# Table entries traced behind the first half of the scores, and the last tile but one taken down before the last goes up

## The chip, the cores and the metric

The kernel runs as one program on one core of one Trainium2 chip. The metric is the device time of one execution in microseconds (us); for a kernel it is given as the median of its runs. Before the change the median of three runs is 1698.82 us (1694.02 to 1705.58). The execution that was profiled is a run of its own: it took 1695.92 us, of which the span from the first to the last instruction is 1694.1 us.

## The reference, cut to what matters

One layer of a hybrid model in float32, on x of shape (2, 2048, 256):

```python
x = x + mamba(layernorm(x))        # state-space mixer; not touched by the change
x = x + ffn(layernorm(x))          # 8 experts, each token goes to 2 of them
x = x + attention(layernorm(x))    # 16 heads of 64
x = x + ffn(layernorm(x))          # the same experts again

def attention(x, w_qkv, w_out, ln_w, ln_b):   # cut
    x_in = layer_norm(x, ln_w, ln_b)
    q, k, v = split(x_in @ w_qkv.T)
    attn = softmax(einsum('ibnd,jbnd->ijbn', q, k) / sqrt(256), axis=1)
    return x + einsum('ijbn,jbnd->ibnd', attn, v) @ w_out.T

def ffn(x, Wr, br, Wl1, bl1, Wl2, bl2):       # cut
    s = x @ Wr.T + br                          # router: best 2 of 8, weights from a softmax
    a, b = split(x @ Wl1[e] + bl1[e])          # for each chosen expert e
    y = (silu(a) * b) @ Wl2[e] + bl2[e]        # summed with the two weights
```

Attention runs over the first axis of x, which has length 2: every token attends to itself and to the token at the same place in the other sequence. A softmax over two values is a sigmoid of their difference, and that is how the kernel computes it.

## The kernel before, in words

**Stages.** In order of time: the mixer with the routing and the first tiles of the first expert layer (to about 741 us), the remaining tiles of the first expert layer (tiles named `_f`, to about 897 us), attention together with the routing and the first tiles of the second expert layer (tiles named `_g` and, for the early ones, `_ge`; to about 1408 us), and the remaining tiles of the second expert layer (to the end at 1694.1 us).

**Experts.** The class `Experts` serves both expert layers: `ffn` for the first, whose results are added into `resid`, and `last` for the second, whose results are added into the output. For each group of 512 tokens, `prepare` takes the layer norm, writes the tokens (`acc`, L316) and their normalized rows (`xnd`, L318) to memory through the SP queue, and works out which expert slots each token gets. `enter` then writes one table row of three numbers for each token and slot by indirect DMAs on POOL: 16 "free" blocks once (L420, the first time only), and 8 blocks for each group (L433), each block being 128 rows. Each entry may not be issued before the last POOL instruction named by `pool(...)` (`tc.issue_after(on_pool[0])`), and the entries of L433 wait for all 16 free ones. When some groups are in, `plan_early` decides on VectorE (DVE) which expert tiles are already full, and `early` may run those before all groups are in. A tile is 256 tokens of one expert; a half tile is 128.

**One expert tile.** `fetch` has SP load the table rows (L656) and the expert's weights and biases (L668 to L674), and POOL gathers the tokens (L683). `turn` transposes the tokens on TensorE (PE; L709) and copies them on ScalarE (ACT; L713). `up` runs four parts (`up_part`: matmuls at L722, a silu on ACT at L730, a product on DVE at L731 into `gT`). `down` multiplies `gT` with the second weight (L754), takes bias and gate into `y` (ACT L766, DVE L767) and adds the two halves of `y` to memory by indirect DMAs on POOL (L778); between the two halves a gather of a later tile or a small memset (L777) is issued. `by` (L766) has one buffer, the banks of `down` (tag C) are two.

**The late tiles** are run by `run`. In its loop tile i goes up, tile i+1 is turned, and tile i-1 is taken down. At its end, with n the number of tiles, the last tile goes up in four parts and the last but one is taken down between part 1 and part 2 (`between`), then the last is taken down. In the second expert layer the last but one is a full tile, in the first it is a half tile.

**Attention** works on four steps s of 512 tokens in each of the two sequences. For each s: `front` (layer norms and transposes), `scores` (eight pieces of query and key products, L1337, with DVE products and sums at L1356 and L1357), `weights` (sigmoid, transposition `ppt` at L1372, a store of the probabilities to memory at L1377 and eight loads `o<-prob` of 512 KB each, which spread them over the partitions, L1383), `mix` (value products `pvd`, L1411, each multiplied on DVE with `o`, L1419) and `outward` (output products `pao`, L1431, added to x on DVE, L1439). The first half of `scores(s+1)` stands between `weights(s)` and `mix(s)`, the second half behind `outward(s)`.

**What sets the order.** The side work (`front`, `prepared`, `entered`) are generators in a list, `aside.waiting`; the main loop takes a few steps of the first one in the list at fixed places (`aside.step`). A generator that has to wait spins there: `front(s+2)` yields without work until `mix(s)` has been traced, and while it does, nothing behind it in the list moves. What is written this way is the order in which the program is traced. In attention only the SP queue keeps that order; on PE, DVE, ACT and POOL a planner lists the instructions ahead of time: of those that are ready by its own estimates, the one traced first goes first. In `run`, POOL, ACT and DVE keep the written order too, and only PE is listed by the planner.

For each s the list gets, behind what it still holds, the generator `entered()`, which writes the table entries of all groups that are routed by the time it is reached, and plans early tiles behind the fourth and the sixth group. Groups are numbered 1 to 8, two for each s.

Of the kernel before, what the change touches and what calls it, by code (L numbers as in the profile page):

```python
# [46 lines left out]
def kernel(  # L47
# [35 lines left out]
    def bank(tag, name):  # L83
        return ps.tile([P, 512], F32, tag=tag, name=name)
# [140 lines left out]
    aside = Aside()  # L225
# [54 lines left out]
    class Experts:  # L280
# [451 lines left out]
                t["gT"][:, i, :n], p[:, n : 2 * n], t["b1"][:, NHT + i : NHT + i + 1], sa[:, :n], ALU.add, ALU.mult  # L732
            )

        def up(self, i, between=None):
            t = self.ts[i]
            nm = t["nm"]
            pool = fe if i % 2 else self.f2
            t["gT"] = pool.tile([P, NHT, TT], F32, tag="gT", name=f"gT_{nm}", bufs=1)
            for j in range(NHT):  # L740
                self.up_part(t, j, "AB"[j % 2])
                if between is not None and j == 1:
                    between()

        def down(self, i, tag, then):
            t = self.ts.pop(i)
# [67 lines left out]
        def run(self):  # L814
            ahead = 3
            first = next(i for i, t in enumerate(self.seq) if not t[4])
            n = len(self.seq)
            with (
                tc.tile_pool(name=f"f2{self.name}", bufs=2) as self.f2,
                tc.manual_schedule(  # L820
                    engines={mybir.EngineType.Pool, mybir.EngineType.Activation, mybir.EngineType.DVE}
                ),
            ):
                self.fetch(first + ahead + 1, first + ahead)
                self.turn(first)
                assert self.seq[-1][1] == 2
                for i in range(first, n - 1):
                    self.fetch(i + ahead + 2, i + ahead + 1, gather=False)
                    if i == first + 6:
                        with tc.manual_schedule(engines={mybir.EngineType.PE}):  # L830
                            beyond = nc.values_load(self.beyond[0:1, 0:1], min_val=0, max_val=NHF - NIN)
                            self.up(i)
                    else:
                        self.up(i)
                    self.turn(i + 1)
                    if i > first:
                        self.down(i - 1, "C", i + ahead)
                    else:
                        for h in range(2):
                            self.gather(i + ahead, h)  # L840
                    if i == first + 2:
                        yield
                self.up(n - 1, lambda: self.down(n - 2, "C", None))
                self.down(n - 1, "C", None)
                with tc.If(beyond > 0):
                    for tile in self.more:
                        i = len(self.seq)
                        self.seq.append(tile)
                        self.fetch(i + 1, i + 1)
                        self.turn(i)  # L850
                        self.up(i)
                        self.down(i, "C", None)
# [5 lines left out]
    with tc.tile_pool(name="ssm1", bufs=1) as s1, tc.tile_pool(name="ssm2", bufs=2) as s2:  # L858
# [315 lines left out]
        for i, (b, s, t) in enumerate(chunks):  # L1174
            j = order.index((b, s)) + 1
# [51 lines left out]
    with tc.tile_pool(name="att1", bufs=1) as a1, tc.tile_pool(name="att2", bufs=2) as a2:  # L1227
# [36 lines left out]
        def entered():  # L1264
            while routed:
                n, group = routed.pop(0)
                if n == len(order):
                    last.plan()
                yield from last.enter(*group)
                if n in EARLY:  # L1270
                    last.plan_early(n, EARLY[n], group[2])
                    tiles.step()
# [56 lines left out]
        def scores(s, ts):  # L1329
            xT, xd = inputs[s]  # L1330
            if s not in sums:
                sums[s] = a2.tile([P, GT, 2, AH], F32, tag="sums", name=f"sums_{s}")

            def proj(tag, j, src, t, half, nm):
                p = bank(tag, nm)
                for k in range(KD):
                    nc.tensor.matmul(  # L1337
                        p,
                        src[:, k, t * P : (t + 1) * P],
                        w_qkv_sb[:, k, j, half * TG : (half + 1) * TG],  # L1340
                        start=(k == 0),
                        stop=(k == KD - 1),
                    )
                return p

            nh = TG // AD
            for t in ts:
                for half in range(AW // TG):
                    nm = f"{s}{t}{half}"
                    pk = proj("A", 1, xd, t, half, f"pk_{nm}")  # L1350
                    kd = a2.tile([P, TG], F32, tag="kd", name=f"kd_{nm}")
                    nc.scalar.mul(kd, pk, SCALE)  # L1352
                    qk = a2.tile([P, 2, TG], F32, tag="qk", name=f"qk_{nm}")
                    for i in range(2):
                        pq = proj("BC"[i], 0, xT[i], t, half, f"pq_{nm}{i}")
                        nc.vector.tensor_tensor(qk[:, i, :], pq, kd, ALU.mult)  # L1356
                    nc.vector.tensor_reduce(  # L1357
                        sums[s][:, t, :, half * nh : (half + 1) * nh],
                        qk.rearrange("p i (h d) -> p i h d", d=AD),
                        AX.X,  # L1360
                        ALU.add,
                    )
                    aside.step(3)
# [42 lines left out]
        def mix(s):  # L1406
            xd, o = inputs.pop(s)[1], mixing[s]
            for c in range(NA):
                pvd = bank("A", f"pvd_{s}{c}")
                for k in range(KD):  # L1410
                    nc.tensor.matmul(  # L1411
                        pvd,
                        w_qkv_sb[:, k, 2, c * P : (c + 1) * P],
                        xd[:, k, :],
                        start=(k == 0),
                        stop=(k == KD - 1),
                    )
                for i in range(2):
                    nc.vector.tensor_tensor(o[i][:, c, :], pvd, o[i][:, c, :], ALU.mult)  # L1419
                if c % 2:  # L1420
                    aside.step(2)
            mixed.add(s)

        def outward(s):
            o = mixing[s]
            for i in range(2):
                for t in range(0, GT, 2):
                    po = bank("C", f"pao_{s}{i}{t}")
                    for j in range(2):
                        for c in range(NA):  # L1430
                            nc.tensor.matmul(  # L1431
                                po[:, j * DM : (j + 1) * DM],
                                o[i][:, c, (t + j) * P : (t + j + 1) * P],
                                w_o_sb[:, c, :],
                                start=(c == 0),
                                stop=(c == NA - 1),
                            )
                    x = xg[i, s][:, t : t + 2, :]
                    nc.vector.tensor_tensor(x, po.rearrange("p (t d) -> p t d", t=2), x, ALU.add)  # L1439

                    aside.step(4 if s == NS - 1 else 2)
                aside.add(prepared(i, s))
                if s == NS - 1 or s == NS - 2 and i:
                    aside.add(entered())
            if s + 3 < NS:
                aside.add(front(s + 3))
# [11 lines left out]
        for s in range(NS):  # L1458

            if s + 1 < NS:  # L1460
                while s + 1 not in inputs:
                    aside.step()
                aside.add(entered())
                scores(s + 1, range(0, GT // 2))
            else:
                aside.rest()
                tiles.step(4)
            mix(s)
            outward(s)
            if s + 1 < NS:  # L1470
                scores(s + 1, range(GT // 2, GT))
                weights(s + 1)
# [68 lines left out]
```

## Time and profile before

| | |
|---|---|
| median of 3 runs | 1698.82 us (1694.02 to 1705.58) |
| profiled execution | 1695.92 us |
| its span, first to last instruction | 1694.1 us |
| outside the span | 1.82 us |
| PE busy | 1584.1 us (94% of the span), 7088 matmuls |
| DVE, POOL, ACT busy | 897.0 us, 736.2 us, 670.9 us |
| moved by DMA | 231.30 MB, mean 137 GB/s |
| mean granted TensorE clock | 0.972 |

The profile is of one execution. A row of a timeline gives the start, the time that the merged instructions took together, the engine (SPq is the SP queue, which only issues transfers), the line, the operation, what is written and read, and how many; in square brackets stands how long the engine was idle before the row and what ended that. A row of stages gives for a stretch of the span its length, then the busy time of PE, PEld (weight loads), DVE, ACT and POOL with the number of instructions, then the granted clock, the mean busy share of the 16 DMA engines, and what they moved. The chain of waits follows the work that ended last back to the start.

### The profile page before, as it was taken

To read this page: it belongs to the slowest core of one execution; us is meant where nothing else is said; L and a number is where in the kernel's file an instruction comes from. 1 tells how busy PE (TensorE), PEld (TensorE's weight loads), DVE (VectorE), ACT (ScalarE), POOL (GpSimd) and SP (SyncE) were. 2 spreads that over 40 slices of the span, in tenths; PEclk is the share of its full clock that TensorE was granted. 3 is DMA by queue.
4 is the path that set the end of the run, shared out by engine and by line. 5 is a ranking of instruction groups with operands and counts; after the bars stand their busy time and mean duration, and the time that the engine had idled before them with its cause. 6 is when DMAs were issued, how large, how long until landed. Compare 5 with 4: busy or idle time off the path is not lost.

```text
span 1694.1 us, 22151 instructions
## 1 busy us (share of the span) xinstructions
PE 1584.1 (94%) x7088; PEld 1193.8 (70%) x7088; DVE 897.0 (53%) x2471; ACT 670.9 (40%) x1338; POOL 736.2 (43%) x702
## 2 busy tenths in 40 slices
PE   6997988989989989999998999899999999999997
PEld 4664555677766777788885566475767878888886
DVE  6778878837648464422226757547554622222222
ACT  4886867856647543222332201101020322333322
POOL 2356357455555566634442002422240663544443
PEclk9898988999989999999999999999999999999999
DMA  4112202742535455889852231706435588888883
GB/s 157 38 54 60 88 28 61 215 126 61 168 63 160 125 144 131 209 244 320 230 133 82 54 72 52 100 13 139 144 62 150 147 215 240 222 231 229 230 215 48
DMA packets 174744, 231.30 MB, mean 137 GB/s; under 512 B 45920, under 2 KB 138080, under 8 KB 174368
## 3 DMA queue, kind: packets, MB, share of 16 engines
q1 hardware_dynamic: 143520, 193.42, 38.9%
q0 software_dynamic: 31104, 36.42, 12.0%
q8 instruction: 58, 0.95, 0.2%
q14 instruction: 62, 0.51, 0.1%
HBM read 192.72 MB, written 37.06 MB: 136 GB/s over the span
## 4 chain that ended last, share of the span: by engine, by line
PE 66%; DVE 12%; DMA 11%; POOL 5%; ACT 3%; issue 3%; SPq 1%; DVEq 0%; POOLq 0%; ACTq 0%
PE pab_g L722 9%; PE pao L1431 7%; PE pab_fe L722 5%; PE pq L1337 5%; PE pab_f L722 5%; PE pf_g L754 4%; PE pf_fe L754 4%; PE pab_ge L722 3%; DVE xc L1007 3%; PE pk L1337 3%; PE pvd L1411 3%; PE pi L1103 2%; DMA lb<-sums 2%; PE pc L990 2%; PE pf_f L754 2%
## 5 line engine op out<-in xcount | busy, mean ns | idle before, releaser
L722 PE MATMUL pab_g<-xT_g,w_g 128*128 128x256 f32 (+1 forms) x896 | 181.6, 361 | 0.0
L722 PE MATMUL pab_fe<-xT_fe,w_fe 128*128 128x256 f32 x672 | 157.8, 390 | 20.0 <-DVE gT_fe L731 17.1
L722 PEld LDWEIGHTS pab_g<-xT_g,w_g 128*128 128x128 f32 x896 | 158.5, 191 | 19.4 <-ACT xT_g L713 0.4
L722 PEld LDWEIGHTS pab_fe<-xT_fe,w_fe 128*128 128x128 f32 x672 | 128.5, 194 | 46.9 <-DVE gT_fe L731 21.8
L778 POOL DMA_INDIRECT out_dram<-y_g,tab_g x51 | 80.3, 1575 | 137.4 <-DVE y_g L767 57.9
L730 ACT ACTIVATE sa_g<-pab_g,b_g 128x256 f32<-128x256 f32 (+1 forms) x112 | 50.9, 454 | 191.3 <-PE pab_g L722 191.3
L731 DVE SCALAR_TENSOR_TENSOR gT_g<-pab_g,b_g,sa_g 128x256 f32<-128x256 f32 (+1 forms) x112 | 51.5, 460 | 129.0 <-ACT sa_g L730 129.0
L1337 PE MATMUL pq<-w_qkv_sb,axT 128*128 128x512 f32 x256 | 117.1, 597 | 0.0
L1007 DVE SCALAR_TENSOR_TENSOR xc<-pre,conv_w_sb,xc 128x512 f32<-128x512 f32 x144 | 113.3, 796 | 6.0 <-ACT xc L999 5.4
L1431 PE MATMUL pao<-w_o_sb,o 128*128 128x256 f32 x512 | 112.3, 380 | 0.0
L1431 PEld LDWEIGHTS pao<-w_o_sb,o 128*128 128x128 f32 x512 | 97.1, 190 | 15.8 <-issue 2.6
L433 POOL DMA_INDIRECT table_g<-pay_g,at_g x64 | 62.7, 980 | 86.2 <-DVE w_g L409 52.7
L990 PE MATMUL pc<-xT,w_in_sb 128*128 128x512 f32 x192 | 97.4, 638 | 0.4 <-ACT xc L999 0.4
L722 PE MATMUL pab_f<-xT_f,w_f 128*128 128x256 f32 (+1 forms) x512 | 96.6, 347 | 0.0
L754 PE MATMUL pf_g<-w_g,gT_g 128*128 128x256 f32 x408 | 92.9, 380 | 0.0
L722 PEld LDWEIGHTS pab_f<-xT_f,w_f 128*128 128x128 f32 x512 | 85.5, 191 | 9.4
L1044 ACT ACTIVATE lt<-lb,cum 128x128 f32<-128x128 f32 x256 | 82.8, 394 | 19.0 <-DMA lb<-sums 19.0
L1337 PEld LDWEIGHTS pq<-w_qkv_sb,axT 128*128 128x128 f32 x256 | 48.6, 192 | 58.8 <-issue 57.4
L1352 ACT ACTIVATE kd<-pk 128x512 f32<-128x512 f32 x32 | 19.1, 597 | 162.4 <-PE pk L1337 96.0
L778 POOL DMA_INDIRECT resid<-y_fe,tab_fe x42 | 67.0, 1595 | 37.5 <-DVE y_fe L767 21.9
L731 DVE SCALAR_TENSOR_TENSOR gT_fe<-pab_fe,b_fe,sa_fe 128x256 f32<-128x256 f32 x84 | 39.7, 480 | 80.5 <-ACT sa_fe L730 80.4
L754 PE MATMUL pf_fe<-w_fe,gT_fe 128*128 128x256 f32 x336 | 80.3, 392 | 2.2 <-DVE gT_fe L731 2.2
(477 smaller groups left out, 3368.6 us busy)
## 6 DMA issues: line engine op xcount, KB each, us to landing
w_g<-in_wl_dram SPq DMA_DIRECT2D x28, 1024.0 KB
w_fe<-in_wl_dram SPq DMA_DIRECT2D x21, 1024.0 KB
lb<-sums SPq DMA_DIRECT2D x32, 512.0 KB
w_f<-in_wl_dram SPq DMA_DIRECT2D x16, 1024.0 KB
o<-prob SPq DMA_DIRECT2D x32, 512.0 KB
w_g<-in_wl_dram SPq DMA_DIRECT2D x28, 512.0 KB
w_fe<-in_wl_dram SPq DMA_DIRECT2D x21, 512.0 KB
w_ge<-in_wl_dram SPq DMA_DIRECT2D x9, 1024.0 KB
```

What stands on the lines that cost most here:

```text
L433: i = nc.gpsimd.indirect_dma_start(out=self.table, out_offset=bass.IndirectOffsetOnAxis(ap=at[:, t, c : c + 1], axis=0), in_=pay[:, t, c, ...
L722: nc.tensor.matmul(p[:, q * n : (q + 1) * n], t["w1"][:, k, c * P : (c + 1) * P], t["xT"][:, k, :], start=(k == 0), stop=(k == KD - 1),)
L730: nc.scalar.activation(sa[:, :n], p[:, 0:n], AF.Silu, bias=t["b1"][:, i : i + 1])
L731: nc.vector.scalar_tensor_tensor(t["gT"][:, i, :n], p[:, n : 2 * n], t["b1"][:, NHT + i : NHT + i + 1], sa[:, :n], ALU.add, ALU.mult)
L754: nc.tensor.matmul(pos[h][:, h * DM : (h + 1) * DM], t["gT"][:, j, h * P : (h + 1) * P], t["w2"][:, j, :], start=(j == 0), stop=(j == NHT ...
L778: j = nc.gpsimd.indirect_dma_start(out=self.acc if self.direct else self.acc[: self.seq[i][4] or NT + TT, :], out_offset=bass.IndirectOffs ...
L990: nc.tensor.matmul(pc, w_in_sb[:, k, DI + c * P : DI + (c + 1) * P], xT[:, k, :], start=(k == 0), stop=(k == KD - 1),)
L1007: nc.vector.scalar_tensor_tensor(xc[:, c, :], pre[:, c, j : j + TG], conv_w_sb[:, c, j : j + 1], xc[:, c, :], ALU.mult, ALU.add,)
L1044: nc.scalar.activation(lt[:, i, :], lb[:, i, :], AF.Relu, bias=g["cum"][:, t, i : i + 1], scale=-1.0)
L1337: nc.tensor.matmul(p, src[:, k, t * P : (t + 1) * P], w_qkv_sb[:, k, j, half * TG : (half + 1) * TG], start=(k == 0), stop=(k == KD - 1),)
L1411: nc.tensor.matmul(pvd, w_qkv_sb[:, k, 2, c * P : (c + 1) * P], xd[:, k, :], start=(k == 0), stop=(k == KD - 1),)
L1431: nc.tensor.matmul(po[:, j * DM : (j + 1) * DM], o[i][:, c, (t + j) * P : (t + j + 1) * P], w_o_sb[:, c, :], start=(c == 0), stop=(c == NA ...
```

## The change

```diff
-        def up(self, i, between=None):
+        def up(self, i):
...
             for j in range(NHT):
                 self.up_part(t, j, "AB"[j % 2])
-                if between is not None and j == 1:
-                    between()
...
-                self.up(n - 1, lambda: self.down(n - 2, "C", None))
+                self.down(n - 2, "C", None)
+                self.up(n - 1)
                 self.down(n - 1, "C", None)
...
             if s + 1 < NS:
                 while s + 1 not in inputs:
                     aside.step()
-                aside.add(entered())
                 scores(s + 1, range(0, GT // 2))
+
+                aside.waiting.insert(0, entered())
             else:
                 aside.rest()
                 tiles.step(4)
             mix(s)
```

**In both expert stages** the last tile but one is taken down as a whole before the last tile starts to go up. Until now two of the four parts of the last tile went up ahead of it.

**In attention** `entered()` is now made behind the first half of `scores(s+1)`, and it is put at the head of the list in place of its end. From there on nothing else in the list moves until the entries of the groups routed by then are traced.

Followed through the steps of the list, this means: at s=0 no group is routed, and nothing differs. At s=1 the entries of groups 1 and 2 (with the free ones) are traced through `mix(1)` and `outward(1)`, where `front(3)` used to spin and then to finish; they used to stand behind it, from `outward(1)` through the second half of `scores(2)`. `front(3)` finishes behind them. As the spinning steps are no longer lost, `prepare` of groups 3 and 4 is traced some ten steps earlier: all of group 3 in the second half of `scores(2)`, and group 4 as far as its normalized rows there and the rest at `weights(2)` and at the start of the first half of `scores(3)`; before, group 3 had only its statistics ahead of `weights(2)`, and the rest of both groups stood in the first half of `scores(3)`. At s=2 the entries of groups 3 and 4 are traced from `mix(2)` to `outward(2)` (before: from the end of the first half of `scores(3)` to `mix(2)`), followed by the early plan. From the second block of `outward(2)` on the traced order is the same.

## The prediction

> **What bounds the kernel now.** I read the page first, then the table of stages around the change, then, for the stages where PE waits, the chain of waits and the timelines of POOL and SP.
>
> ```profile
> span 1694.1 us, 22151 instructions
> PE 1584.1 (94%) x7088; PEld 1193.8 (70%) x7088; DVE 897.0 (53%) x2471; ACT 670.9 (40%) x1338; POOL 736.2 (43%) x702
> ```
>
> ```profile
> 1060.00:1098.00 38.00, 31.13 (x75) 13.81 (x75) 19.47 (x30) 3.73 (x6) 15.32 (x16) 0.91 0.84 111
> 1098.00:1250.00 152.00, 152.00 (x591) 101.48 (x589) 91.20 (x281) 16.25 (x30) 44.90 (x46) 1.00 0.33 83
> 1250.00:1288.00 38.00, 35.49 (x135) 24.27 (x134) 15.89 (x35) 7.03 (x13) 11.10 (x11) 1.00 0.83 179
> 1288.00:1413.00 125.00, 118.26 (x580) 101.94 (x579) 52.45 (x194) 32.31 (x62) 61.55 (x52) 1.00 0.64 176
> ```
>
> PE is the bound. Its idle time by stage (length less PE's busy time) is 6.9 us around mix(1), 0 from 1098 to 1250, where nearly all that the change reorders lies, 2.5 at mix(3) and 6.7 behind it. A new order can win only from these idle times; where PE is full it merely permutes PE's work. The wait at mix(1), in the chain, then on POOL, then on SP:
>
> ```profile
> 1069.62 24.37 DMA o<-prob
> 1094.09 0.70 DVE o L1419
> ```
>
> ```profile
> 1050.64 1.63 POOL L1290 TENSOR_TENSOR rs_l<-rs_l,mhalf 128x8 f32<-128x8 f32 x1 [5.30 <-DVE rs_l L1289]
> 1052.45 1.06 POOL L420 DMA_INDIRECT table_g<-rest_g,free  x1 [0.17 <-issue]
> ...
> 1167.32 1.03 POOL L433 DMA_INDIRECT table_g<-pay_g,at_g  x1 [37.76 <-DVE w_g L409]
> ```
>
> ```profile
> 1055.29 0.32 SPq L1377 DMA_DIRECT2D prob<-prow  x1
> 1059.26 11.47 SPq L1383 DMA_DIRECT2D o<-prob  x8
> ...
> 1150.56 0.33 SPq L1377 DMA_DIRECT2D prob<-prow  x1
> 1152.32 5.81 SPq L1383 DMA_DIRECT2D o<-prob  x8
> ```
>
> To be seen: mix(1) waits for the loads of o, which take 34.8 us (1059.26 to 1094.09). And the free entries start on POOL at 1052.45, right behind the POOL instruction that they are tied to (it ends at 1052.27), although they are traced only in outward(1), which PE reaches at 1098.5. The planner has already hoisted them as far as the tie allows.
>
> The end of the second expert stage on POOL: second add of the last tile but two, then two adds of the last but one, then the first of the last (its second is at 1685.40).
>
> ```profile
> 1672.21 1.57 POOL L778 DMA_INDIRECT out_dram<-y_g,tab_g  x1 [0.19 <-issue]
> 1677.26 1.56 POOL L778 DMA_INDIRECT out_dram<-y_g,tab_g  x1 [3.48 <-DVE y_g L767]
> ...
> 1679.12 1.57 POOL L778 DMA_INDIRECT out_dram<-y_g,tab_g  x1 [0.19 <-issue]
> 1683.54 1.55 POOL L778 DMA_INDIRECT out_dram<-y_g,tab_g  x1 [2.85 <-DMA out_dram<-y_g,tab_g]
> ```
>
> The add at 1677.26 waits for its y. The one at 1683.54 waits for the add before it to land: 4.42 us from issue to next issue. Two halves of a tile are 1.86 us apart.
>
> **Part 1: the tails of both expert stages.** Nothing is added or removed. 16 matmuls of the last tile but one (3.45 us) swap with two up parts of the last (3.45 us), so PE ends when it did; POOL's order stays. In the second layer y of the last but one comes 3.45 us sooner (DVE from 1673.0, not 1676.5), so its first add is held by the landing alone: 1672.21 + 4.42 = 1676.63, not 1677.26. The rest follows at 1678.49, 1682.91 and 1684.77, not 1685.40; the last y's (DVE ends 1682.22 and 1683.96) are there by then. Gain 0.6 us. In the first layer the last but one is a half tile: its add (886.07) already stands 4.45 us behind the add at 881.62, with y ready at 884.65. Gain 0. Behind the moved work, ACT's bias product waits until DVE frees `by` (1670.47) and is through by 1671.4; the first silu queued behind it is wanted at 1669.34 + 3.45 + 1.73 = 1674.5. If that cover of 3.1 us were gone, at most 3.1 us a stage would be lost.
>
> **Part 2, s=1.** The free entries and those of groups 1 and 2 keep tie, data and an otherwise empty POOL. Tracing an instruction earlier changes nothing when it already runs at its earliest: 0. The wait at mix(1) stays; with the slower clock behind it (16 pvd took 8.67 us where 6.9 is usual) it costs 8.6 us. Were the tie no hindrance, I could be wrong by all of that. front(3)'s difference, now traced behind the entries, ran on DVE at 1099.78 and is read by PE at 1150.5: 50 us of cover.
>
> **Part 2, s=2, groups 3 and 4 prepared earlier.** A group costs PE 0.87 (transposes) + 1.69 (router) + 0.36 (small products) = 2.9 us wherever it stands. Group 3's now precede weights(2), so ppt moves from 1149.4 to 1152.3, while mix(2) still starts at 1177.5. The cover between them shrinks from 28.1 to 25.2 us, and to 22.6 if 2.6 us of group 4 get ahead of ppt too; at s=0 it was 22.1 (959.2 to 981.3) and sufficed. Behind ppt: the store of prob at 1153.5; its landing after 1.8 (1150.56 to 1152.32) to 4.0 us (1055.29 to 1059.26); so loads from 1155.3 to 1157.5. At s=0 all eight took 21.6 us (962.2 to 983.8), half of them 10.8. Then the first half is there at 1166 to 1168 (DVE wants it at 1179.6), the second at 1177 to 1179 (wanted at 1184.4). Cost 0, 5 us of cover left.
>
> SP: three stores (xnd of group 3, x and xnd of group 4) pass ahead of prob and the loads. The last needs an xn that DVE ended at 1131.0, and prob is due at 1153.5: no wait, and 1.5 MB less beside the loads. DVE takes some 5 us for group 3 into 24 us of which 14.7 are busy: hidden.
>
> **Part 2, s=2, the entries.** Group 3's first entry came 8.1 us behind its router product (1159.2 to 1167.3), group 4's 9.6 (1172.6 to 1182.2). Now the eight of group 3 (1.26 us each) come at about 1153 to 1163 and those of group 4 at 1165 to 1175. The early plan, its table loads (1194.0) and gathers follow some 15 us sooner; PE reads the first at 1249.1, so that wins nothing. But all 16 entries now lie over the loads of o. Three stretches of such loads, by their last column (GB/s), without entries, with free ones, and with those of group 3:
>
> ```profile
> 967.00:972.00 5.00, 5.00 (x13) 2.28 (x12) 1.57 (x3) 1.31 (x3) 0.00 (x0) 1.00 1.06 211
> 1065.00:1070.00 5.00, 5.00 (x13) 2.26 (x12) 2.60 (x3) 0.60 (x1) 3.56 (x4) 1.00 0.71 64
> 1167.00:1172.00 5.00, 5.00 (x28) 3.28 (x26) 2.92 (x6) 1.07 (x2) 3.77 (x4) 1.00 1.05 210
> ```
>
> Free entries slow the loads (34.8 us in place of 21.6); group entries, four in that stretch, do not (210 against 211). The moved ones are of the second kind, so I take 0; the other end is a second wait like that at mix(1), 8.6 us.
>
> A rule speaks against the change here: the Trainium skill, "DMA: Bandwidth & Descriptors", section "Specifications", puts the smallest transfer at full rate at 512 B and has smaller writes read, modified and written back. An entry writes 128 rows of 12 B, so by the page 16 entries would move as much as 16 x 128 x 2 x 512 B = 2.1 MB, an estimate that at 205 GB/s makes 10 us more for the loads and some 5 us for the sum. The stretch at 1167 does not bear it out, the one at 1065 does.
>
> **Sum.** -0.6 (part 1) + 0 + 0 + 0: 1695.92 - 0.6 = 1695.3 for the profiled execution (span 1694.1 and 1.82 outside), which lies 2.9 us below the median of the runs shown. On the median: 1698.8 - 0.6 = 1698.2.
>
> **The rivals.**
> A wait at mix(2): the moved entries slow the loads of o as the free ones did. For it: they lie over the whole load, as at s=1. Against it: 210 GB/s at 1167. First half after 25.4 us (1059.26 to 1084.70), at 1180.7 to 1182.9; it decides once that is later than 1179.6. Price 8.6 us: 1706.8, slower than before.
> The entries do move at s=1, off the loads: these take 21.6 us and the wait at mix(1) goes, -8.6: 1689.6. For it: that wait is the largest in attention. Against it: the tie.
> The planner lists PE anew and two of its covers fail, 2 x 8.6 us: 1715. For it: everything behind 1126 is listed anew. Against it: PE's work there is the same, and full.
> All idle time of attention goes (16.1, 1.8 of clock, 0.6): 1680. Nothing in the trace says why mix(3) or the early tiles behind it should improve.
>
> **How the numbers follow.** Forecast 0.70, wait at mix(2) 0.14, entries off the loads at s=1 0.06, two covers lost 0.07, all idle gone 0.03. The forecast's own range is the spread of the runs before less 0.6, 1693 to 1705. For 8 in 10 the last two cases are left out and the next two taken in, with some of that spread above: 1689 to 1711. A difference of 1% (17 us) is about what can be told from none. Slower by over 1%: two covers lost 0.07 and an enlarged wait at mix(2) 0.03; faster: 0.03 and 0.01 of the spread; within: 0.86.
>
> **What would show it.** Right: free entries again at some 2 us behind the tie and a wait of 6 to 7 us at mix(1); entries of group 3 from about 1153; pvd of mix(2) without idle time; the last add 0.6 us sooner against the last matmul. Wrong: an idle PE between 1177 and 1192, loads of o at s=2 above 22 us, a mix(1) without a wait, or PE idle in the tails.

## The result and the profile after

| | before | after |
|---|---|---|
| median of 22 runs each, same chip | 1699.26 us (1692.98 to 1707.21) | 1697.72 us (1689.03 to 1706.63) |
| ratio after to before | | 0.9986, 95% interval 0.9972 to 1.0001 |
| profiled execution, span | 1694.1 us | 1702.0 us (a run of 1703.7 us) |

No change that a measurement of this kernel can tell from none: the forecast of 1698.2 us was 0.5 us off the median. That it came so close is luck: it started from a median of three runs, and the interval of the ratio is some 2.5 us wide to each side. The profiled execution after is one of the longer of the 22 runs. Its 6 extra us against the median show at the passage from the early to the late tiles, where PE waited 7.8 us for gathers (`xs_g`) and 1.7 us before. The profiles below that keep the change there show 1.1 to 1.8 us in that place, so this is not the change.

The page of after, head and busy times:

```profile
span 1702.0 us, 22149 instructions
PE 1585.8 (93%) x7088; PEld 1194.0 (70%) x7088; DVE 896.3 (53%) x2471; ACT 674.6 (40%) x1340; POOL 739.0 (43%) x702
```

The table of stages of after (length, busy time of PE, PEld, DVE, ACT, POOL, granted clock, DMA share, GB/s):

```profile
1060.00:1098.00 38.00, 31.74 (x77) 14.54 (x76) 19.97 (x32) 3.06 (x5) 14.61 (x16) 0.91 0.77 111
1098.00:1250.00 152.00, 152.00 (x588) 100.72 (x587) 91.11 (x285) 20.41 (x34) 45.97 (x47) 1.00 0.32 83
1250.00:1288.00 38.00, 35.85 (x137) 24.83 (x136) 15.52 (x29) 5.59 (x12) 9.98 (x9) 1.00 0.81 179
```

Length less PE's busy time gives 6.3, 0 and 2.2 us of idle PE, against 6.9, 0 and 2.5 before. PE has the same 7088 matmuls, and where the order changed it is full both times.

POOL's timeline of after: the instruction to which the free entries are tied, the first of these, then the first entries of groups 3 and 4.

```profile
1049.69 1.63 POOL L1289 TENSOR_TENSOR rs_l<-rs_l,mhalf 128x8 f32<-128x8 f32 x1 [5.30 <-DVE rs_l L1288]
1051.49 1.06 POOL L420 DMA_INDIRECT table_g<-rest_g,free  x1 [0.17 <-issue]
...
1152.71 1.03 POOL L433 DMA_INDIRECT table_g<-pay_g,at_g  x1 [25.06 <-DVE w_g L409]
...
1166.73 0.95 POOL L433 DMA_INDIRECT table_g<-pay_g,at_g  x1 [4.11 <-DVE w_g L409]
```

The free entries start where they did, 1.8 us behind the start of the tied instruction. Only the entries of groups 3 and 4 moved: they stood at 1167.3 and 1182.2. SP's queue and PE's rows at mix(1) and mix(2):

```profile
1054.32 0.32 SPq L1376 DMA_DIRECT2D prob<-prow  x1
1058.46 10.51 SPq L1382 DMA_DIRECT2D o<-prob  x8
...
1153.82 0.32 SPq L1376 DMA_DIRECT2D prob<-prow  x1
1157.55 6.13 SPq L1382 DMA_DIRECT2D o<-prob  x8
```

```profile
1074.74 3.60 PE L1410 MATMUL pvd<-axd,w_qkv_sb 128*128 128x512 f32 x8
1084.60 12.04 PE L1410 MATMUL pvd<-axd,w_qkv_sb 128*128 128x512 f32 x24 [6.26 <-DVE o L1418]
...
1175.58 10.53 PE L1410 MATMUL pvd<-axd,w_qkv_sb 128*128 128x512 f32 x24
1185.94 0.59 PE L1430 MATMUL pao<-w_o_sb,o 128*128 128x256 f32 x2
1186.37 3.60 PE L1410 MATMUL pvd<-axd,w_qkv_sb 128*128 128x512 f32 x8
```

At mix(1) PE still waits 6.3 us for DVE, which waits for the loads of o. At mix(2) no bracket stands behind any row: PE never stood there, although 16 entries now lie over the loads. At the end of the kernel the adds of the last three tiles (POOL):

```profile
1678.66 1.56 POOL L776 DMA_INDIRECT out_dram<-y_g,tab_g  x1 [6.75 <-DVE y_g L765]
...
1685.04 1.56 POOL L776 DMA_INDIRECT out_dram<-y_g,tab_g  x1 [2.95 <-DMA out_dram<-y_g,tab_g]
...
1693.24 1.57 POOL L776 DMA_INDIRECT out_dram<-y_g,tab_g  x1 [0.19 <-issue]
```

The add at 1685.04 no longer waits for its `y` but for the landing of the add before it. From the first of these adds to the last it is 14.58 us, and it was 15.05 (1670.35 to 1685.40): 0.47 us gained. Over all profiles of this document it is 14.58 to 14.76 us in the eleven kernels with the new tails and 15.05 to 15.39 in the three without.

### The profile page after: what moved, and what is told of

Read it like the earlier page. It is cut to its first block, busy times and chain, and to the rows that moved or that the text cites. A ratio compares the mean times of both kernels' runs of the same rounds, so it can differ in the third digit from the quotient of the medians.

```text
span 1702.0 us, 22149 instructions
## 1 busy us (share of the span) xinstructions
PE 1585.8 (93%) x7088; PEld 1194.0 (70%) x7088; DVE 896.3 (53%) x2471; ACT 674.6 (40%) x1340; POOL 739.0 (43%) x702
## 4 chain that ended last, share of the span: by engine, by line
PE 46%; DMA 7%; DVE 1%; issue 1%; POOL 1%; SPq 0%; ACT 0%; DVEq 0%; POOLq 0%
PE pab_g L722 9%; PE pao L1430 7%; PE pq L1336 6%; PE pab_f L722 5%; PE pf_g L752 4%; PE pvd L1410 3%; PE pab_ge L722 3%; PE pk L1336 3%; DMA out_dram<-y_g,tab_g 2%; PE pf_f L752 2%; DMA o<-prob 2%; PE pf_ge L752 1%; PE pr_g L330 1%; DMA xs_f<-xnd_f,tab_f 1%; DMA resid<-y_f,tab_f 1%
## 5 line engine op out<-in xcount | busy, mean ns | idle before, releaser
L722 PEld LDWEIGHTS pab_g<-xT_g,w_g 128*128 128x128 f32 x896 | 158.4, 190 | 19.6 <-ACT xT_g L713 0.4
L776 POOL DMA_INDIRECT resid<-y_fe,tab_fe x42 | 67.0, 1595 | 38.2 <-DVE y_fe L765 22.6
L752 PEld LDWEIGHTS pf_g<-w_g,gT_g 128*128 128x128 f32 x408 | 75.4, 190 | 9.3 <-DVE gT_g L731 0.2
```

The source lines that it names most:

```text
L722: nc.tensor.matmul(p[:, q * n : (q + 1) * n], t["w1"][:, k, c * P : (c + 1) * P], t["xT"][:, k, :], start=(k == 0), stop=(k == KD - 1),)
L752: nc.tensor.matmul(pos[h][:, h * DM : (h + 1) * DM], t["gT"][:, j, h * P : (h + 1) * P], t["w2"][:, j, :], start=(j == 0), stop=(j == NHT ...
L776: j = nc.gpsimd.indirect_dma_start(out=self.acc if self.direct else self.acc[: self.seq[i][4] or NT + TT, :], out_offset=bass.IndirectOffs ...
```

## The experiments

My theory: the change does nothing because its large part cannot move what costs time. The free entries keep their place behind their tie, and there they slow the loads of o, which is what PE waits for at mix(1). The rivals: each part has an effect and the two cancel; the wait at mix(1) has another cause; the moved entries at s=2 come close to a new wait at mix(2). All ratios are to the kernel before on the same chip. Its median there was 1720.0 us for the first four kernels, 1725.7 for the next three, and 1700.4 and 1700.2 for the rest, so times are compared only as ratios.

| kernel | ratio | 95% interval |
|---|---|---|
| the tails alone | 0.9998 | 0.9981 to 1.0015 |
| the entries alone | 0.9989 | 0.9971 to 1.0006 |
| all entries from s=2 on | 1.0167 | 1.0144 to 1.0191 |
| no free entries | 0.9978 | 0.9959 to 0.9997 |
| one free entry behind mix(1) | 1.0015 | 0.9999 to 1.0031 |
| all entries from s=2 on, four buffers | 1.0100 | 1.0073 to 1.0128 |
| entries of groups 3 and 4 twice | 1.0090 | 1.0074 to 1.0105 |
| before, again | 0.9996 | 0.9977 to 1.0016 |
| free entries untied | 1.0001 | 0.9977 to 1.0025 |
| untied, groups 1 and 2 behind mix(1) | **0.9958** | 0.9937 to 0.9979 |
| all 32 behind mix(1) | 1.0089 | 1.0054 to 1.0123 |
| free entries between the scalings | **0.9967** | 0.9943 to 0.9991 |

### Each part alone

The tails alone: the first two hunks of the diff without the third.

> Part 1 alone: the last tile but one is taken down first, attention keeps the order of before. My theory (PE is full wherever the change reorders it, and only the chain of adds at the end moves): 0.5 us less than before, ratio 0.9997, and between the first add of the last tile but two and the last add of the kernel 14.6 us in place of 15.05. Rival 'two effects cancel' (one part wins several us and the other loses them): this run is at least 5 us, 0.3%, away from before.

The entries alone: the third hunk without the first two.

> Part 2 alone: entries traced behind the first half of the scores and ahead of what else waits, the tails as before. My theory: POOL issues all entries in the order of before, the free ones 2 us behind the instruction that they are tied to, so mix(1) waits 6 to 7 us as before; mix(2) has no idle time although its cover is 3 us shorter; ratio 1.000 within 0.2%. Rival 'two effects cancel': at least 5 us, 0.3%, away from before, on the other side than the tails alone. Rival 'entries slow the loads at s=2': loads of o at s=2 above 25 us and PE idle in mix(2).

Neither part differs from the kernel before by more than its interval, some 3 us to each side, so two effects of 5 us that hide each other are ruled out. In the trace, first of those last adds to last took 14.76 us with the tails alone and 15.28 with the entries alone: some 0.5 us again, too little for the clock of whole runs to show.

### The free entries away from the loads: all entries from s=2 on

```diff
-                aside.waiting.insert(0, entered())
+                if s == 2:
+                    entries = entered()
+                    for _ in range(16):
+                        next(entries)
+                    aside.waiting.insert(0, entries)
```

> The changed kernel, but no entries are traced at s=1: at s=2 the free entries and those of groups 1 and 2 are traced at once behind the first half of scores(3), so they are tied to the POOL instruction of group 4's layer norm (about 1119 us) and lie behind the loads of o at s=1. My theory (the wait at mix(1) is made by the free entries lying over these loads): loads of o at s=1 take 22 us in place of 34, PE is idle less than 1 us in mix(1), and the kernel is 8 us faster than the changed one, ratio to before 0.994 to 0.996. Rival 'the loads at s=1 are slow for another reason' (their issue, the landing of prob): loads still above 30 us, ratio 0.9986. Rival 'the wait only moves': the entries of four groups now lie over the loads of o at s=2, these take above 30 us and PE is idle 5 to 9 us in mix(2), ratio 0.998 to 1.000.

The wait at mix(1) went: between 1060 and 1098 PE was busy for all 38.00 us, and all 32 `pvd` ran without idle time.

```profile
1060.00:1098.00 38.00, 38.00 (x111) 18.79 (x110) 28.03 (x56) 5.53 (x9) 1.64 (x1) 1.00 0.54 113
```

But the kernel became 1.7% slower. PE's timeline, then DVE's, of this kernel:

```profile
1156.12 0.60 PE L363 MATMUL pk_g<-sel_g,tri 128*128 128x32 f32 x2 [7.95 <-DVE sel_g L357]
...
1185.21 3.78 PE L1392 MATMUL pv<-w_ov,axT 128*128 128x256 f32 x8 [19.55 <-DVE qk L1355]
```

```profile
1176.94 0.17 DVE L391 TENSOR_TENSOR at_g<-lo_g,hi_g 128x4 int32<-128x4 f32 x1 [19.61 <-DMA table_g<-pay_g,at_g]
...
1177.09 0.69 DVE L1355 TENSOR_TENSOR qk<-pq,kd 128x512 f32<-128x512 f32 x1
```

DVE stood 19.6 us before it could write the slots of a group (`at`, two buffers), because the late entries of the group two before had not yet read them. The products `qk` queue behind it on DVE, and PE behind these. Not all of the loss need lie there: this profile also has 44.5 us of waits on DVE and ACT that nothing in the trace releases (last section).

### The same with four buffers for the slots

```diff
-            at = rt2.tile([P, GT, 2], I32, tag="at", name=f"at_{nm}")
+            at = rt2.tile([P, GT, 2], I32, tag="at", name=f"at_{nm}", bufs=4)
```

> The kernel with all entries at the third quarter (ratio 1.0167), and four buffers instead of two for the positions that DVE writes and the entries read. If the new wait of 30 us there came from DVE standing behind these buffers, the products and PE behind it, the two gaps of PE (7.95 us before the counts of group 3, 19.55 us before the products with w_ov) go, and with the wait at mix(1) gone too the ratio is 0.994 to 0.999. If they came from the entries on POOL or from the slowed loads themselves, the ratio stays above 1.01. In between: 48 entries in a row lie over the loads of the third quarter, which may bring back 5 to 9 us at mix(2): ratio 0.999 to 1.004.

```profile
1158.94 0.17 DVE L389 TENSOR_REDUCE lo_g<-slot_g 128x4 f32<-128x32 f32 x1
...
1159.22 0.15 DVE L391 TENSOR_TENSOR at_g<-lo_g,hi_g 128x4 int32<-128x4 f32 x1
```

DVE writes the slots at once and 1.0167 becomes 1.0100, so the buffers were a part of it, not all. The rest is idle time between 1144 and 1205 (PE 32.3 us busy of the 50 from 1150) that this trace does not explain; see the section on what was not expected.

### No free entries

The call that makes the 16 free entries is left out.

> The changed kernel without the 16 free entries of the second expert layer (they are left out; the empty places of a first tile then carry their first table rows, with weight zero). The 16 entries of groups 1 and 2 then start at once, at about 1052 us, and lie over the loads of o at s=1 from their first to their last byte. My theory (group entries do not slow the loads, free ones do): loads of o at s=1 take 22 to 24 us, PE idle in mix(1) below 1 us, ratio to before 0.994 to 0.996. Rival 'any small entry slows the loads': loads above 30 us, the wait at mix(1) of 5 us or more stays, ratio 0.998 to 1.000.

PE's rows around mix(1):

```profile
1080.50 1.98 PE L1327 MATMUL pk<-w_qkv_sb,axd 128*128 128x512 f32 x4 [1.15 <-issue]
1084.14 3.70 PE L1327 MATMUL pq<-w_qkv_sb,axT 128*128 128x512 f32 x8 [1.66 <-DVE qk L1346]
...
1092.16 7.13 PE L1401 MATMUL pvd<-axd,w_qkv_sb 128*128 128x512 f32 x16 [0.88 <-DVE o L1409]
1100.01 3.70 PE L1401 MATMUL pvd<-axd,w_qkv_sb 128*128 128x512 f32 x8 [0.71 <-DVE o L1409]
```

1.6 us are left of the wait at mix(1), and 2.8 us of waits stand just ahead of it (the first two rows), beside 3.7 us in which ACT stood with nothing in the trace that releases it. The gain of 0.2% is below the price of the whole wait. The entries of groups 1 and 2, no longer held back by the free ones, now lie over the loads: the stretches 1075 to 1080 and 1080 to 1085 moved 152 and 166 GB/s. So group entries slow loads too at this place, which the prediction denied for the other.

### Entries twice at s=2

Groups 3 and 4 are entered a second time, into a table that nobody reads: `yield from last.enter(*group)` again with `last.table` exchanged.

> The changed kernel, with the 16 entries of groups 3 and 4 made twice, the second time to a table that nobody reads: 32 entries of POOL instead of 16 lie over the loads of the third quarter. The prediction had a rival in which the entries that the change moves over these loads make PE wait at mix(2) (8.6 us). In the profile of after there was no wait there. If the cover of about 5 us that the prediction gave is right, the doubled entries (about 18 us more of them, at a loss of some 0.4 us of load for each us of entries) bring a wait of 2 to 5 us at mix(2), ratio 1.000 to 1.003; if the loads are not slowed by group entries, there is no idle time at mix(2) and the ratio is that of after, 0.998 to 1.000.

Slower, and with waits at mix(2), but not by the rival's mechanism. The loads of o, issued at 1172.1, were through at about 1196 by the transfer rates: 24 us, where after took 23. PE's waits come later:

```profile
1202.95 7.13 PE L1415 MATMUL pvd<-axd,w_qkv_sb 128*128 128x512 f32 x16 [3.26 <-DVE o L1423]
...
1215.67 3.78 PE L1415 MATMUL pvd<-axd,w_qkv_sb 128*128 128x512 f32 x4 [3.44 <-issue]
```

From 1196 until it took up the products with `o` at 1201.6 DVE was busy with other work, and before the row at 1214.33 it stood 4.63 us with nothing in the trace that released it. As a test of the doubled entries the run is weak: those of group 4 came only from 1193.0 on, so 15 entries were issued while the loads ran, and in after 12. Why it lost 0.9% stays open.

### The free entries behind mix(1)

The first try made one free entry wait for the last product of mix(1), in the belief that the others queue behind it.

```diff
+                        if not self.freed:
+                            tc.add_manual_dep(i.ins, self.behind.name, ...)
...
+            if s == 1:
+                last.behind = product.ins
+                aside.waiting.insert(0, entered())
```

> The changed kernel, with the first of the 16 free entries made to wait for the last product of mix(1) on DVE, so that all 32 entries of the second quarter start behind the loads of o instead of over them; the entries of groups 3 and 4 stay where the change put them. If the free entries are what makes PE wait at mix(1) (6.3 us in the profile of after), and the 20 us of delay does no harm elsewhere (the kernel with all entries at the third quarter lost 30 us because DVE could not write the positions of groups 3 and 4 before the entries of groups 1 and 2 had read theirs), then the wait at mix(1) is under 1 us, the window 1060 to 1098 is full, and the time is 6 to 9 us below the kernel before (ratio 0.9945 to 0.997). The rival is that the entries find something else to wait for or to delay (DVE's positions, the gathers that read the table): then the ratio is 0.998 or more and the trace shows the idle time behind 1098.

```profile
1083.19 0.96 POOL L420 DMA_INDIRECT table_g<-rest_g,free  x1 [4.62 <-DMA table_g<-rest_g,free]
1111.29 1.16 POOL L420 DMA_INDIRECT table_g<-rest_g,free  x1 [27.14 <-DVE o L1425]
```

It did not do what it was meant to. The entries are free of order among themselves, the planner let 15 pass ahead, and the wait stayed (1.28 and 5.56 us at mix(1)). The second try put the dependency on all 16; the group entries follow them.

> The changed kernel, with all 32 entries of the second quarter made to wait for the last product of mix(1); the earlier try had this wait on one free entry alone, and 15 others went ahead of it over the loads, so that the wait of 6.8 us stayed. If the free entries over the loads make the wait, it is gone here as at the kernel with all entries at the third quarter (window 1060 to 1098 full), and the ratio is 0.994 to 0.997 if nothing else is late. The rival: POOL has 40 us of entries and landings to do behind 1098, the scalings of groups 3 and 4 (rs_g) queue behind them some 20 to 30 us later than now, and PE stands at their transposes: ratio 1.000 to 1.01, with the idle time between 1110 and 1190.

```profile
1140.20 1.38 DVE L248 TENSOR_SCALAR xn_g<-x,mv_g,rs_g 128x256 f32<-128x256 f32 x4 [36.11 <-POOL rs_g L244]
```

```profile
1142.23 3.78 PE L1342 MATMUL pq<-w_qkv_sb,axT 128*128 128x512 f32 x4 [22.84 <-DVE x L1447]
```

The rival's case. The loads ran at 211 to 212 GB/s, mix(1) had no wait (38.00 of 38.00 us busy), but POOL was taken from 1090.0 until 1139.1, the scaling `rs_g` of group 3 stood behind that, DVE stood 36.1 us for it, and PE 22.8 us for DVE.

This kernel also gives the price of the wait. From `ppt` of s=0 to the first `pao` of outward(1) PE took 130.3 us (957.89 to 1088.17), as in the two kernels with all entries from s=2 on; before it is 139.1 us (959.23 to 1098.37), after 138.2. The wait costs some 8.9 us, and it was lost again behind outward(1).

### The kernel before once more

> The kernel before, unchanged, profiled on the chip of these runs. The profiles of the last experiments show waits that nothing in the trace releases (DVE and ACT idle for 5 to 24 us between 1100 and 1420, with DMA engines nearly idle in some), and the profiles of before and after, taken on another chip, show none; times on this chip are 1.2 to 1.6% longer for every kernel. If these waits belong to the chip and the run, this profile shows some of them too (5 us or more in the sum over DVE and ACT between 1030 and 1420); if they come from the edits of the experiments, it shows none, as the first profile of before. Ratio 1.000 in either case, within 0.002.

The ratio is 0.9996, DVE and ACT have no wait without a releaser, and the wait at mix(1) is 6.7 us. The chip was another than those of the first seven runs, one on which the kernel takes 1700 us and not 1720 or more, so the question put to this run is answered only by the comparison over chips further down.

### Free entries untied, and the version that is faster

The positions of the free entries are known to DVE at 1034.5 in after, 17 us before the tie lets them start.

```diff
-                        with tc.issue_after(on_pool[0]):
-                            i = nc.gpsimd.indirect_dma_start(
+                        i = nc.gpsimd.indirect_dma_start(
```

> The changed kernel, in which the 16 free entries no longer stand behind the instruction of POOL that was the last when they were traced: 13 of them go ahead of the two scalings of the third front (rs_l), from when their positions are known, and so ahead of the store of the weights at mix(1) and of the loads of o. Behind them the 16 entries of groups 1 and 2 come free about 17 us sooner and lie over the loads, as in the kernel without free entries (ratio 0.9978, waits of 1.6 us left at mix(1) and 2.8 before it). If it is the entries over the loads that make the wait at mix(1), it falls from 6.3 to between 1 and 3 us and the ratio is 0.996 to 0.9985. The rival: the two scalings come about 9 us later and PE waits for the transposes of that front, which gives the gain back: ratio 0.999 to 1.004.

Two kernels more keep that and hold the entries of groups 1 and 2 until the last product of mix(1), by a dependency on each of the 16; the second of them also writes out POOL's order, five free entries, a scaling, five, a scaling, six (`m` counts the free entries made so far, and `on_pool` now keeps the last two of the POOL instructions named by `pool(...)`):

```diff
+                        m = len(self.freed)
+                        with tc.issue_after(on_pool[m < 10]) if m > 4 else ExitStack():
```

> As the untied kernel, and each of the 16 entries of groups 1 and 2 waits for the last product of mix(1), so that neither kind lies over the loads of o at the second quarter. If entries of both kinds slow the loads, the wait at mix(1) is under 1 us and the ratio is 0.994 to 0.997, below the untied kernel's by 0.001 to 0.002. If only free entries matter, it is that of the untied kernel. If the scalings of the third front, 9 us late, cost PE what is gained, both are 0.999 or more.

> As the kernel with untied free entries and held group entries (ratio 0.9958), but POOL's order is written so that the two scalings of the third front (rs_l) are not late: five free entries go ahead of the first, five between the two, six behind the second. In the untied kernel these scalings came some 9 us late and PE waited 3.3 us at the transposes of the weights and 0.6 us at the next products with w_qkv; the wait at mix(1) was gone. Now the scalings start within 2 us of when they did before (after the first profile's 1042.8 and 1049.7), the two waits of 3.9 us go, and the last six free entries lie beside the store of the weights and the start of the loads, which brings back at most 1 to 2 us at mix(1): ratio 0.993 to 0.9965. The rival: the six entries slow the loads as much as 16 did and the wait of 5 to 6 us at mix(1) is back, ratio 0.998 or more.

PE's rows of the first, untied alone:

```profile
1056.33 0.61 PE L1370 MATMUL ppt<-ident,sums 128*32 128x128 f32 x4 [3.17 <-ACT sums L1366]
...
1084.99 7.13 PE L1409 MATMUL pvd<-axd,w_qkv_sb 128*128 128x512 f32 x16 [1.13 <-DVE o L1417]
1094.91 5.26 PE L1409 MATMUL pvd<-axd,w_qkv_sb 128*128 128x512 f32 x8 [2.79 <-DVE o L1417]
```

Of the second, with the group entries held, first PE's rows, then one stretch of its loads in the table of stages:

```profile
1056.99 0.61 PE L1377 MATMUL ppt<-ident,sums 128*32 128x128 f32 x4 [3.25 <-ACT sums L1373]
...
1082.82 13.96 PE L1416 MATMUL pvd<-axd,w_qkv_sb 128*128 128x512 f32 x32
```

```profile
1075.00:1080.00 5.00, 5.00 (x13) 2.27 (x12) 2.60 (x3) 0.45 (x2) 0.00 (x0) 1.00 1.06 213
```

Of the third:

```profile
1053.50 0.60 PE L1379 MATMUL ppt<-ident,sums 128*32 128x128 f32 x4
...
1079.37 7.13 PE L1418 MATMUL pvd<-axd,w_qkv_sb 128*128 128x512 f32 x16 [0.32 <-DVE o L1426]
1089.25 5.15 PE L1418 MATMUL pvd<-axd,w_qkv_sb 128*128 128x512 f32 x8 [2.75 <-DVE o L1426]
```

Untied alone, the wait at mix(1) falls from 6.3 to 3.9 us, and the scalings, the first of which now stands behind 13 entries (1051.4 for 1042.8), cost 3.2 us at `ppt`: nothing is won. With the group entries held too, mix(1) has no wait and the loads run at 211 to 213 GB/s; the 3.2 us at `ppt` stay, and the kernel is 0.42% faster than before. With the scalings nearly in time (1043.5 and 1051.5), the wait at `ppt` is gone and 3.1 us at mix(1) are back, since six entries lie beside the store and the start of the loads. Both beat before, and after by their medians' ratios (0.9958 and 0.9967 against 0.9986; the intervals overlap); between the two nothing is decided.

That the wait at mix(1) is made by entries over the loads is shown by the traces: it is gone in all four kernels that keep every entry off them. The gain is less well accounted for. From `ppt` of s=0 to the first `pao` of outward(1) it is 137.6 us in the second kernel and 135.3 in the third, against 139.1 before. So of the third's 5.6 us (interval 1.5 to 9.7) the trace shows 3.9, and 0.5 at the tails; of the second's 7.1 us (3.6 to 10.7) it shows only 1.6 and 0.3, since its waits at `ppt` and the slow clock behind them (last section) took most of what the wait had cost. Where the rest of the 7.1 lies is open.

## Why the prediction was right, point by point

**PE is full where the order changes.** Right: 152.00 of 152.00 us between 1098 and 1250 both times. From the first `pao` of outward(1) to the first `pvd` of mix(2) it is 79.1 us after (1096.47 to 1175.58) and 78.9 before.

**Part 1: 0.6 us in the second layer, 0 in the first.** Measured 0.47 between the adds of one trace each, 0.5 between the two single-part kernels. The two landings took 4.52 and 4.48 us from issue to next issue where 4.42 had been put in for each, which is what is missing. The clock of whole runs cannot confirm a gain of this size. In the first layer the last four adds are 4.6, 4.5 and 2.5 us apart, and were 4.5, 4.5 and 2.5. ACT's bias product held nobody up.

**Part 2, s=1: the tie holds the free entries, so 0.** Right, and the untied kernel confirms it from the other side: without the tie POOL starts them at 1035, and only then does the wait move.

**Part 2, s=2: the store 3 us later, still no wait at mix(2).** `ppt` was put at 1152.3 and came at 1152.1, the store at 1153.5 and came at 1153.8, its landing at 1.8 to 4.0 us and took 3.7, the entries of group 3 at about 1153 and came at 1152.7. mix(2) ran without idle time. But these times agree by two shifts that cancel: after runs 1.9 us ahead of before here (outward(1) began at 1096.47, was 1098.37), and `ppt` stands 55.65 us behind that, was 50.82: 4.8 us later and not the 2.9 of group 3. The cover from `ppt` to mix(2) was 23.5 us, between the 25.2 of the sum and the 22.6 given for a part of group 4 ahead. The loads took some 23 us, and above 22 had been named as a sign of being wrong. They were slowed by some 1.4 us, where the sum had none, and the cover took it up. SP's earlier stores and DVE's earlier work on group 3 cost nothing.

**"Free entries slow the loads; group entries do not".** Half wrong as a rule, right for the place where it was used. At s=2 the loads ran at 204 to 212 GB/s from 1165 on under entries of groups 3 and 4 (with a slower start: some 23 us in all against 21.6 without entries at s=0), and at 213 and 216 GB/s under such entries in the kernel with four buffers. At s=1 the entries of groups 1 and 2 brought them to 152 and 166 GB/s (no free entries) and 166 and 146 (untied). One stretch had been read as a rule on the kind of entry. It is not settled what tells the two places apart; what was seen is that both slow cases are entries of groups 1 and 2.

**The page on small writes.** The Trainium skill, "DMA: Bandwidth & Descriptors", section "Specifications", has the DMA read, modify and write back where a write is under 512 B; counting 512 B twice for each 12-byte write, I had estimated 10 us more for loads under 16 entries. At s=1 the loads took 34.8 us before, and about 21 us in the kernel at 0.9958, which holds all entries off them (issued from 1066.2, through at about 1087 by the transfer rates): 14 us, somewhat above that estimate. At s=2 they took some 23 us in after (1157.6 to about 1180), 1.4 more than at s=0, with 12 entries issued while they ran and four just ahead. The measurement there decides, and the rule alone does not give the price.

**The rivals.** "The entries move off the loads at s=1" did not happen by the change. Its price, put at 8.6 us, is right: 8.9 us are gone up to outward(1) where all entries come later. "A wait at mix(2)" did not come by the change. In the doubled kernel there were two, of 3.26 and 3.44 us, with the loads through before both. Two covers lost, and all idle time gone: neither was seen.

## What to carry to other kernels

Before crediting a reordering, look whether the moved instruction already runs as early as its ties allow; then writing it earlier in the program changes nothing, and the tie or the dependency is what has to change. Look at what a group of many tiny writes lies over and what it stands ahead of. Here, putting all entries later, putting all behind mix(1) and putting the free ones earlier each removed or shortened one wait and made another, and only the free entries earlier together with the group entries later paid; at mix(2) entries over the loads made no wait at all. An instruction moved later takes its inputs' buffers with it: count the buffers that its producer will want.

## What the runs showed of the hardware that was not expected

**The store behind the entries.** At mix(1) the 64 KB store of `prob` landed in 1.7 us when no entries were outstanding (SP's next issue behind it, in the kernels that put all entries later), in 4.1 us in after, and in 4.9 to 6.4 us in four kernels with entries ahead of it. In the kernel at 0.9958 the last free entry had been issued before the store (1056.7 and 1060.3), and the store still took 5.9 us. The landings of the entries themselves vary too: those of the free ones in after took from 3.0 to 17.0 us, 13.4 in the median.

**Idle PE, slow PE.** After some of its waits PE's next matmuls are slow. In the kernel at 0.9958 eight `pq` took 6.57 us behind the waits at `ppt` where 3.60 is usual, with a granted clock of 0.50 between 1060 and 1065: the slow clock cost 3.0 us on top of 3.9 us of waits. Eight `pvd` took 5.26 and 5.15 us behind waits of 2.79 and 2.75 us (untied, and with the scalings between). But behind the 3.26 us of the doubled kernel 16 `pvd` took 7.13 us, as behind a wait of 0.32, at a granted clock of 1.00. The length of the wait alone does not tell, and these runs give no rule.

**Waits without a releaser.** In all seven profiles from the two chips on which the kernel before took 1720 us and more, DVE and ACT stand between 1030 and 1420 for 8 to 86 us in the sum with nothing in the trace that releases them, with the tails alone too (20.4 us); in the profiles from the chips at 1699 to 1700 us there are none, in seven profiles. So they seem to go with the chip and not with an edit, though the kernel before was not profiled on the slower two, and they were longest, 45 to 86 us, in the three kernels with the most entries at s=2. Their cause was not found, and parts of the 1.7% and 1.0% that the two kernels with all entries from s=2 on lost, and of the 0.9% of the doubled entries, may lie in them.
